# Row factors of a four-layer graph attention kernel: turned on TensorE ahead of DRAM, with a new set of due times

## The chip, the core and the metric

The kernel runs on one core of one Trainium2 chip. A core has five engines with a queue each: TensorE (PE in the profile, with its weight loads as PEld), VectorE (DVE), ScalarE (ACT), GpSimd (POOL) and SyncE (SP, which here only issues DMAs). The metric is the device time of one execution, in microseconds (us), as the median of the runs; lower is better. All data is float32.

## What is computed

Eight graphs (b = 0 to 7) of 2048 nodes with 128 channels share one symmetric 0/1 adjacency matrix. Four layers follow each other, and each is added to its input x:

```
h = relu(layernorm(x))
layer 0: Wh = h @ W.T;  s1 = Wh @ a1;  s2 = Wh @ a2
         e[i,j] = leaky_relu(s1[i] + s2[j], 0.2), only where adj[i,j] > 0
         x += elu(softmax(e) @ Wh)
layer 1: the same with Wh = h @ W and no elu
layer 2: 4 heads of 32 channels, scores = h_i . h_j, masked softmax, x += softmax @ h
layer 3: h scaled by node weights, Wh layer-normed, attention as in layer 0,
         x += elu(softmax(e) @ Wh + Wh)
```

In layers 0, 1 and 3 the score is a sum of one number of node i and one of node j, so exp(leaky_relu(s1 + s2)) is a maximum of two products. The kernel needs one factor per node as a column (a number for each partition) and another as a row that lies on all 128 partitions. This row is the "row factor" of the title.

## The kernel before

**Units and the two kinds of work.** There are 32 units, one per graph and layer. Layers 0, 1 and 3 are `Gat` units, layer 2 is a `Heads` unit. Both begin with a prelude: mean and variance of x (`moments`), normalised rows (`rows_made`, ACT), transposes on PE (`transposes`), and for a `Gat` unit the projections and `put` or `put3`, which leave the values `y` and the factors `cr` in SBUF.

The main work of a `Gat` unit is 32 *tokens* (two halves of the target nodes by 16 blocks of source nodes). One token is a DVE instruction `front` (line 718: maximum of the row factors `r` and a column of `cr`, times the edges) and a `back` on PE (line 727: 8 products of 128x128 by 128x129, which the profile counts as 16 matmul instructions). Three buffers `zg` lie between the two. In all there are 768 tokens.

The main work of a `Heads` unit is 64 *beats* (4 heads by 16 blocks): four score matmuls on PE (line 994), two exponentials on ACT (line 1001), a mask on DVE (line 1007) and a weighing on PE (line 1016), mostly for two beats at once. Five buffers `z` hold the beats, and two pairs of PSUM banks ("pair") are shared by the scores, all transposes and all projections. In all there are 512 beats.

**How the row factor gets to all partitions.** `spread` ends a `Gat` unit's prelude. `self.cr[:, 1, :]` holds 128 partitions by 16 numbers; node n*128+p lies on partition p, column n. For 21 of the 24 `Gat` units, `write` (line 667) sends it by DMA to a row of 2048 numbers in DRAM. `targets` (line 698) later reads each half of that row back onto all 128 partitions as `r`, by two DMAs for a unit; the first `front` of a half needs its `r`. The other three units, (0,0), (0,1) and (7,3), spread the row by PE transposes and ACT copies without DRAM (lines 650 and 659), and are not touched. A second way by DRAM stands in the code behind the flag `ROWS_TURNED` (lines 669 to 687).

**What sets the order.** The instruction order of each engine is written out ahead by a planner (`Plan`). Each `Op` has an engine, an estimated duration, needs, slots it takes and frees, a `lag` until others can use its result, and a `due` time. The planner goes through an estimated execution; among the operations of an engine that can start within `WINDOW_US` of the earliest one it takes the one with the lowest due. `HURRY_US` moves fronts ahead while more than one `zg` is free. Due times come from three tables: `TOKENS` (start and step for each unit and half; its order is also the order of all tokens, each bound to the one before it), `BEATS` (start and step for each graph and head; beats, too, are bound in one sequence), and `LEADS` (how long before its start a unit's prelude begins). `EARLY` shifts the kinds of operations against each other. `GATES` holds the tokens of unit (6,3) until named beats of graph 7. The tables give priorities, not times on the chip: waits on the chip come only from data, buffers and queue order.

SP issues in planned order as well: x loads, adjacency loads, the `halves` and `values` of a `Heads` unit to DRAM (lines 898 and 919) and back (933, 939, 944), row writes, row reads and the output. An SP instruction that waits holds up all behind it.

Of the kernel before, what the change touches and what calls it, by code (L numbers as in the profile page):

```python
# [20 lines left out]
P = 128  # L21
# [19 lines left out]
def adj_preln_d4(ctx: ExitStack, tc: tile.TileContext, x, adj, w0, a0, w1, a1, w3, a3,  # L41
# [114 lines left out]
            self.needs = [n for n in needs if n is not None]  # L156
            self.got, self.end, self.users, self.ready = {}, None, [], 0.0

    HURRY_US, WINDOW_US, BEAT_SUMS_US = 89.3, 0.131, 0.86

    EARLY = dict(front=-87.0, score=211.3, exp=171.0, mask=-122.3, sums=-168.7)

    SINGLY = (7,)
    FIRST_ALONE = 4
    DIRECT, ROWS_TURNED, L1_ACT, L3_DMA, L3_OUT = ((0, 0), (0, 1), (7, 1), (7, 2)), False, False, False, False
    PLUS_US, PLUS_LAG_US, GATHER_US, GATHER_LAG_US = 1.0, 5.5, 2.2, 6.5

    class Plan:
# [71 lines left out]
    def fast(ctx):  # L240
# [186 lines left out]
        class Unit:  # L427
# [15 lines left out]
            def moments(self, name, part, rows, needs):  # L443

                key = {}

                def stats(op, q):
                    if q == 0:
                        key["st"] = stat.tile([P, NB, 6], F32, tag="st", name="st")
                    for n in range(q * 4, q * 4 + 4):  # L450
                        nc.vector.bn_stats(out=key["st"][:, n, :], in_=rows()[:, n, :])  # L451

                def begin(op):
                    key["total"], key["v"] = moments_begin(stat, name, key["st"])

                def power(op):
                    key["rstd"] = moments_power(stat, name, key["v"])

                def end(op):
                    key["nmr"] = moments_end(stat, name, key["total"], key["rstd"])  # L460

                if (self.b, self.layer) == (0, 0):
                    return self.first_moments()
                last = []
                for q in range(4):
                    last = [add("DVE", 0.72, self.due(part + 0.03 * q), lambda op, q=q: stats(op, q),
                                last + list(needs[q]))]
                last = [add("DVE", 0.5, self.due(part + 0.11), begin, last)]
                last = [add("POOL", 3.4, self.due(part + 0.12), power, last)]
                return key, [add("DVE", 0.09, self.due(part + 0.14), end, last)] * 4  # L470

            def first_moments(self):

                key, ready = {}, []

                def stats(op, half):
                    if half == 0:
                        key["st"] = stat.tile([P, NB, 6], F32, tag="st", name="st")
                        key["rstd"] = stat.tile([P, NB], F32, tag="rstdx", name="rstdx")
                        key["nmr"] = stat.tile([P, NB], F32, tag="nmrx", name="nmrx")  # L480
                    for n in range(half * HB, (half + 1) * HB):
                        nc.vector.bn_stats(out=key["st"][:, n, :], in_=X[0][:, n, :])
                    sl = slice(half * HB, (half + 1) * HB)
                    key["total", half], key["v", half] = moments_begin(stat, "x", key["st"][:, sl, :])

                def power(op, half):
                    sl = slice(half * HB, (half + 1) * HB)
                    nc.gpsimd.tensor_tensor(out=key["rstd"][:, sl], in0=key["v", half], in1=neg_half[:, sl], op=OP.pow)

                def end(op, half):  # L490
                    sl = slice(half * HB, (half + 1) * HB)
                    nc.vector.scalar_tensor_tensor(key["nmr"][:, sl], key["total", half], -0.5, key["rstd"][:, sl],
                                                   op0=OP.mult, op1=OP.mult)

                for half in range(2):
                    last = add("DVE", 1.9, half, lambda op, half=half: stats(op, half), self.after)
                    last = add("POOL", 3.4, half, lambda op, half=half: power(op, half), [last])
                    last = add("DVE", 0.09, half, lambda op, half=half: end(op, half), [last])
                    ready += [last] * 2
                return key, ready  # L500
# [44 lines left out]
        class Gat(Unit):  # L545
# [92 lines left out]
            def spread(self):  # L638
# [30 lines left out]
                if ROWS_TURNED:  # L669
# [3 lines left out]
                        nc.tensor.transpose(ps[0:NB, op.got["pair"], :P], self.cr[:, 1, :], ident)  # L673

                    def copy_rows(op):
                        key["r"] = stat.tile([NB, P], F32, tag="rt", name="rt", bufs=2)
                        nc.scalar.copy(key["r"], ps[0:NB, turned.got["pair"], :P])

                    def write_rows(op):
# [206 lines left out]
        class Heads(Unit):  # L886
# [172 lines left out]

        GATES = {(6, 3, 0): (7, 10), (6, 3, 1): (7, 48)}  # L1060
        TOKENS = {
            (1, 0, 0): (97.6, 6.88), (0, 1, 0): (73.5, 14.16), (0, 1, 1): (550.6, 7.34),
            (1, 0, 1): (1660.4, 7.3), (2, 0, 0): (1689.5, 7.62), (2, 0, 1): (1764.4, 9.18),
            (1, 1, 0): (430.5, 13.69), (1, 1, 1): (1072.7, 7.7), (3, 0, 0): (1245.7, 8.98),
            (3, 0, 1): (1288.7, 8.31), (2, 1, 0): (1760.1, 7.68), (2, 1, 1): (872.6, 3.08),
            (0, 3, 0): (1689.1, 7.43), (0, 3, 1): (1912.1, 10.3), (3, 1, 0): (2530.9, 14.04),
            (4, 0, 0): (1726.7, 7.6), (3, 1, 1): (1682.5, 8.06), (4, 0, 1): (1756.3, 7.23),
            (1, 3, 0): (1633.1, 3.91), (1, 3, 1): (1288.3, 6.99), (4, 1, 0): (1701.6, 7.25),
            (4, 1, 1): (2745.4, 9.07), (5, 0, 0): (1716.2, 8.46), (5, 0, 1): (1683.8, 9.5),
            (2, 3, 0): (1952.7, 2.05), (2, 3, 1): (2876.6, 8.01), (5, 1, 0): (3026.3, 4.35),  # L1070
            (5, 1, 1): (3255.9, 7.54), (6, 0, 0): (3217.4, 3.78), (6, 0, 1): (3228.0, 6.29),
            (3, 3, 0): (3360.5, 9.13), (3, 3, 1): (3610.0, 7.36), (6, 1, 0): (3752.1, 13.03),
            (6, 1, 1): (4083.3, 4.99), (7, 0, 0): (4105.3, 7.44), (7, 0, 1): (4586.2, 9.82),
            (4, 3, 0): (4181.2, 4.29), (7, 1, 0): (4249.1, 11.6), (7, 1, 1): (4504.3, 7.29),
            (4, 3, 1): (4662.4, 11.71), (5, 3, 0): (4541.9, 11.87), (5, 3, 1): (4694.2, 12.84),
            (6, 3, 0): (4390.1, 14.25), (6, 3, 1): (5179.1, 7.43), (7, 3, 0): (5192.3, 8.4),
            (7, 3, 1): (6460.1, 7.89),
        }
        BEATS = {
            (0, 0): (-266.53, 15.11), (0, 1): (-315.14, 21.46), (0, 2): (-14.69, 14.66),  # L1080
            (0, 3): (593.67, 2.8), (1, 0): (-621.42, 13.74), (1, 1): (-215.39, 3.18),
            (1, 2): (-485.77, 7.14), (1, 3): (278.01, 8.1), (2, 0): (678.31, 14.14),
            (2, 1): (886.15, 2.23), (2, 2): (953.01, 2.45), (2, 3): (1726.79, 10.94),
            (3, 0): (-127.35, 10.64), (3, 1): (1129.71, 0.0), (3, 2): (1181.46, 7.17),
            (3, 3): (1316.42, 11.55), (4, 0): (1548.48, 23.99), (4, 1): (2361.91, 1.13),
            (4, 2): (2366.8, 7.55), (4, 3): (2544.1, 8.8), (5, 0): (2510.32, 10.6),
            (5, 1): (2257.53, 0.0), (5, 2): (2962.35, 15.09), (5, 3): (3457.98, 6.48),
            (6, 0): (2333.01, 6.11), (6, 1): (2924.65, 1.75), (6, 2): (3322.16, 3.55),
            (6, 3): (3721.7, 12.09), (7, 0): (2053.35, 4.55), (7, 1): (2736.5, 1.99),
            (7, 2): (3763.83, 3.23), (7, 3): (3926.73, 7.25),  # L1090
        }
        LEADS = {
            (0, 0): 691.08, (1, 0): 439.88, (0, 1): 835.27, (2, 0): 752.06, (1, 1): 991.07,
            (3, 0): 872.93, (2, 1): 1117.92, (0, 3): 876.91, (3, 1): 44.84, (4, 0): 102.77,
            (1, 3): 1841.07, (4, 1): 1823.39, (5, 0): 52.64, (2, 3): 756.18, (5, 1): 646.99,
            (6, 0): 832.07, (3, 3): 413.34, (6, 1): 340.77, (7, 0): 1416.38, (4, 3): 263.35,
            (7, 1): 510.12, (5, 3): 767.47, (6, 3): 756.1, (7, 3): 1090.32, (0, 2): 205.64,
            (1, 2): 1275.92, (2, 2): 878.78, (3, 2): -270.32, (4, 2): -845.43, (5, 2): 647.9,
            (6, 2): -738.75, (7, 2): -534.5,
        }  # L1100

        def planned():
# [18 lines left out]
            def there(b, layer):  # L1121
                if (b, layer) not in units:
                    if layer:
                        there(b, layer - 1)
                    if layer == 2:
                        start = BEATS[b, 0][0]
                        units[b, 2] = Heads(b, 2, start - LEADS[b, 2], start - 14.0)
                        units[b, 2].beats([BEATS[b, h] for h in range(HEADS)])
                    else:
                        start = next(TOKENS[name][0] for name in TOKENS if name[:2] == (b, layer))  # L1130
                        units[b, layer] = Gat(b, layer, start - LEADS[b, layer], start)
# [218 lines left out]
```

## Time and profile before

| | |
|---|---|
| median of 3 runs | 2776.76 us (2772.88 to 2777.48) |
| the profiled execution | 2775.01 us |
| its span, first to last instruction | 2773.2 us |
| granted PE clock over the span | 0.990 of full speed |
| DVE mask, line 1007, x512 | 1169.8 us, 2286 ns each |
| DVE front, line 718, x768 | 971.4 us, 1279 ns each |
| PE back, line 727, x12288 | 1499.0 us busy |
| PE scores, line 994, x2048 | 720.5 us busy |
| PE weighing, line 1016, x4096 | 502.6 us busy |
| ACT exponential, line 1001, x1024 | 1122.8 us, 1114 ns each |
| DMA packets, and those under 512 B | 255513, 185456 |
| DMA queue 1 (issued by SP) | 186784 packets, 156.46 MB, 23.4% of 16 engines |

Busy time of an engine is the time in which at least one of its instructions runs. Matmuls are pipelined, so that a duration of one is longer than the distance between two, and a PE that is busy all the time need not be at its fastest. The span is 1.8 us shorter than the execution's own time, for what lies before the first and behind the last instruction.

### The profile page before, as it was taken

The page shows a single profiled execution, that of the slowest core. Times are in us where ns is not written, and L with a number is a line of the kernel's source. Part 1 is how long each engine was busy: PE and PEld are TensorE (multiplying, and loading weights), DVE is VectorE, ACT ScalarE, POOL GpSimd, SP SyncE. Part 2 cuts the span into 40 slices and gives each one's busy share as a digit, 9 for nine tenths or more (in the row PEclk, how much of TensorE's full clock was granted, in tenths as well). Part 3 has the DMA queues.
Part 4 walks back from the last instruction along what each step waited for, and adds up shares of the span by engine and source line. Part 5 has one row for each costly group of instructions (what it writes and reads, how often), then busy time and mean ns, then how long its engine had stood idle before and what let it go on. Part 6 is the DMA issues. An engine that isn't in the chain of part 4 may idle for free. (4 is left out here: it accounts for less than half of the span.)

```text
span 2773.2 us, 48892 instructions
## 1 busy us (share of the span) xinstructions
PE 2632.3 (95%) x20083; PEld 2024.3 (73%) x20083; DVE 2515.8 (91%) x3323; ACT 1714.9 (62%) x2768; POOL 253.5 (9%) x114
## 2 busy tenths in 40 slices
PE   6999899999998999999999999999999899999987
PEld 6998778757775677877777678786777567665677
DVE  6867798989999899999999999999899899899987
ACT  4333566567666658656767567665676756787651
POOL 2100010011001001001100011010010100010010
PEclk9999999999999999999999999999999999999999
DMA  8005233432224424323333423423324221623000
GB/s 308 17 9 94 60 58 58 92 62 48 78 58 93 56 54 73 66 65 58 54 65 85 80 42 74 79 53 69 62 59 95 46 54 16 122 50 58 12 16 25
DMA packets 255513, 181.78 MB, mean 66 GB/s; under 512 B 185456, under 2 KB 220400, under 8 KB 249136
## 3 DMA queue, kind: packets, MB, share of 16 engines
q1 hardware_dynamic: 186784, 156.46, 23.4%
q0 software_dynamic: 68080, 22.04, 8.3%
q8 instruction: 159, 2.61, 0.4%
q14 instruction: 74, 0.61, 0.1%
q10 hardware_dynamic: 416, 0.07, 0.0%
HBM read 123.03 MB, written 33.73 MB: 57 GB/s over the span
## 5 line engine op out<-in xcount | busy, mean ns | idle before, releaser
L1001 ACT ACTIVATE z<-ps,shift 128x1024 f32<-128x1024 f32 x1024 | 1122.8, 1114 | 725.5 <-PE ps L994 719.5
L727 PEld LDWEIGHTS ps<-y,zg 128*128 128x128 f32 x12288 | 1466.7, 193 | 85.1 <-DVE zg L718 41.2
L727 PE MATMUL ps<-y,zg 128*128 128x129 f32 x12288 | 1499.0, 276 | 31.1 <-DVE zg L718 28.1
L1007 DVE SCALAR_TENSOR_TENSOR z<-z,edge 128x2048 f32<-128x2048 f32 x512 | 1169.8, 2286 | 70.0 <-ACT z L1001 68.6
L718 DVE SCALAR_TENSOR_TENSOR zg<-r,cr,edge 128x1024 f32<-128x1024 f32 x768 | 971.4, 1279 | 119.1 <-PE ps L727 98.3
L994 PE MATMUL ps<-m,s 128*128 128x512 f32 x2048 | 720.5, 438 | 66.2 <-ACT z L1001 55.1
L994 PEld LDWEIGHTS ps<-m,s 128*128 128x128 f32 x2048 | 314.9, 191 | 348.3 <-ACT z L1001 243.6
L1016 PE MATMUL ps<-z,v 128*32 128x512 f32 x4096 | 502.6, 602 | 2.2 <-DVE z L1007 1.8
L1016 PEld LDWEIGHTS ps<-z,v 128*32 128x32 f32 x4096 | 103.1, 109 | 238.6 <-issue 187.0
L511 ACT ACTIVATE h<-x,nmrx,rstdx 128x128 f32<-128x128 f32 x512 | 210.5, 491 | 47.9 <-DVE nmrx L116 31.9
L111 POOL TENSOR_TENSOR rstdx<-varx,neg_half 128x16 f32<-128x16 f32 x31 | 123.2, 3973 | 760.5 <-DVE varx L106 760.5
L1041 POOL DMA_DIRECT2D x<-o x31 | 65.8, 2123 | 838.8 <-DVE o L1036 748.8
L566 PEld LDWEIGHTS ps<-rhs,h_t 128*128 128x128 f32 x768 | 102.0, 199 | 9.2 <-ACT h_t L558 3.7
L566 PE MATMUL ps<-rhs,h_t 128*128 128x130 f32 x768 | 107.1, 285 | 0.3 <-ACT h_t L558 0.3
L451 DVE BATCH_NORM_STATS2 st<-x 128x6 f32<-128x128 f32 x496 | 106.7, 279 | 0.0
L540 PE MATMUL ps<-ident,h 128*128 128x128 f32 x512 | 81.2, 281 | 18.2 <-ACT h L511 11.1
L540 PEld LDWEIGHTS ps<-ident,h 128*128 128x128 f32 x512 | 63.0, 143 | 36.1 <-ACT h L511 13.2
L795 POOL DMA_DIRECT2D x<-oa x26 | 23.5, 903 | 665.4 <-DVE x L789 176.6
L766 ACT ACTIVATE oe<-oa 128x1024 f32<-128x1024 f32 x32 | 33.9, 1060 | 74.0 <-DVE oa L785 63.2
L760 DVE TENSOR_TENSOR oa<-ps,rs 128x384 f32<-128x384 f32 x144 | 73.9, 513 | 5.0
L558 ACT COPY h_t<-ps 128x512 f32<-128x512 f32 x96 | 55.9, 584 | 31.1 <-PE ps L540 31.1
L591 ACT ACTIVATE y<-ps,y 128x128 f32<-128x128 f32 x256 | 73.0, 369 | 0.0
(120 smaller groups left out, 818.9 us busy)
## 6 DMA issues: line engine op xcount, KB each, us to landing
s<-halves SPq DMA_DIRECT2D x256, 128.0 KB, 2.8
m<-halves SPq DMA_DIRECT2D x64, 512.0 KB, 6.9
r<-row SPq DMA_DIRECT2D x42, 512.0 KB, 4.1
raw<-in_adj_dram SPq DMA_DIRECT2D x16, 1024.0 KB, 16.7
x<-oa POOLq DMA_DIRECT2D x26, 512.0 KB, 5.2
values<-h SPq DMA_DIRECT2D x32, 256.0 KB, 2.5
halves<-hi SPq DMA_DIRECT2D x128, 64.0 KB, 1.7
halves<-lo SPq DMA_DIRECT2D x128, 64.0 KB, 1.7
```

The source lines that it names most:

```text
L111: nc.gpsimd.tensor_tensor(out=rstd, in0=v, in1=neg_half, op=OP.pow)
L451: nc.vector.bn_stats(out=key["st"][:, n, :], in_=rows()[:, n, :])
L511: nc.scalar.activation(self.h[q][:, k, :], X[self.b][:, n, :], AF.Relu, scale=key["rstd"][:, n:n + 1], bias=key["nmr"][:, n:n + 1])
L540: nc.tensor.transpose(pk[:, k, :], self.h[q][:, k, :], ident)
L566: nc.tensor.matmul(pv[:, k, :C + 2], lhsT=self.h_t[q][:, k * P:(k + 1) * P], rhs=rhs, start=True, stop=True)
L718: nc.vector.scalar_tensor_tensor(z, self.r[half], self.cr[:, 0, jb:jb + 1], edge[:, jb, half * HN:(half + 1) * HN], op0=OP.max, op1=OP.mult)
L727: nc.tensor.matmul(ps[:, self.banks(half, place)[i // 3], k * CE:(k + 1) * CE], lhsT=z[:, i * P:(i + 1) * P], rhs=self.y[:, jb, :], start= ...
L760: nc.vector.tensor_mul(key["a"][:, i0:i1, :], pv[:, :, :C], r[:, i0:i1, None].to_broadcast([P, i1 - i0, C]))
L994: nc.tensor.matmul(ps[:, lo + c, :], lhsT=self.S[h, jb // HB][:, at:at + P], rhs=self.M[h][:, (c2 * 2 + c) * 512:(c2 * 2 + c + 1) * 512], ...
L1001: nc.scalar.activation(self.z[s][:, c2 * HN:(c2 + 1) * HN], ps[:, lo:lo + 2, :].rearrange("p b t -> p (b t)"), AF.Exp, bias=shift)
L1007: nc.vector.scalar_tensor_tensor(self.z[s], self.z[s], 1.0, edge[:, jb, :], op0=OP.mult, op1=OP.mult, accum_out=self.den[:, h, jb:jb + 1])
L1016: nc.tensor.matmul(ps[c * HD:(c + 1) * HD, 0, :], lhsT=self.V[h][:, jb, :], rhs=z[:, c * 512:(c + 1) * 512], start=jb == 0, stop=jb == NB - 1,
```

## The change

`ROWS_TURNED` becomes True. The 21 units that sent the factors straight to DRAM now transpose them on PE into a PSUM bank (128 partitions by 16 columns become 16 partitions by 128), copy these by ACT into a tile `rt` of [16, 128] and write that. The row in DRAM has the same 2048 numbers in the same places, and the reading is the same. `rt` gets one buffer in place of two, and `st` (the statistics of a prelude) two in place of three. All numbers of `TOKENS`, `BEATS`, `LEADS`, `EARLY`, `HURRY_US` and `WINDOW_US` are new; in `TOKENS` the two halves of unit (2,1) now come ahead of those of unit (3,0), and the rest keeps its order. `there` makes the `Heads` unit of the graph before first, so that beats stay in the order of graphs. `GATES` stays.

```diff
-    HURRY_US, WINDOW_US, BEAT_SUMS_US = 89.3, 0.131, 0.86
-    EARLY = dict(front=-87.0, score=211.3, exp=171.0, mask=-122.3, sums=-168.7)
+    HURRY_US, WINDOW_US, BEAT_SUMS_US = 70.8, 0.139, 0.86
+    EARLY = dict(front=-107.6, score=111.1, exp=-8.6, mask=-164.7, sums=-334.5)
...
-    DIRECT, ROWS_TURNED, L1_ACT, L3_DMA, L3_OUT = ((0, 0), (0, 1), (7, 1), (7, 2)), False, False, False, False
+    DIRECT, ROWS_TURNED, L1_ACT, L3_DMA, L3_OUT = ((0, 0), (0, 1), (7, 1), (7, 2)), True, False, False, False
...
-                        key["st"] = stat.tile([P, NB, 6], F32, tag="st", name="st")
+                        key["st"] = stat.tile([P, NB, 6], F32, tag="st", name="st", bufs=2)
...
-                        key["r"] = stat.tile([NB, P], F32, tag="rt", name="rt", bufs=2)
+                        key["r"] = stat.tile([NB, P], F32, tag="rt", name="rt", bufs=1)
...
         TOKENS = {
-            (1, 0, 0): (97.6, 6.88), (0, 1, 0): (73.5, 14.16), (0, 1, 1): (550.6, 7.34),
-            (1, 0, 1): (1660.4, 7.3), (2, 0, 0): (1689.5, 7.62), (2, 0, 1): (1764.4, 9.18),
-            (1, 1, 0): (430.5, 13.69), (1, 1, 1): (1072.7, 7.7), (3, 0, 0): (1245.7, 8.98),
-            (3, 0, 1): (1288.7, 8.31), (2, 1, 0): (1760.1, 7.68), (2, 1, 1): (872.6, 3.08),
+            (1, 0, 0): (-22.6, 16.91), (0, 1, 0): (53.7, 14.45), (0, 1, 1): (278.3, 12.5),
+            (1, 0, 1): (1550.7, 12.7), (2, 0, 0): (1538.2, 13.82), (2, 0, 1): (1781.1, 13.31),
+            (1, 1, 0): (27.5, 13.73), (1, 1, 1): (467.0, 14.14), (2, 1, 0): (387.8, 14.31),
+            (2, 1, 1): (552.8, 14.26), (3, 0, 0): (1505.8, 15.6), (3, 0, 1): (544.1, 12.33),
...
         BEATS = {
-            (0, 0): (-266.53, 15.11), (0, 1): (-315.14, 21.46), (0, 2): (-14.69, 14.66),
+            (0, 0): (-186.75, 13.08), (0, 1): (-165.33, 21.31), (0, 2): (148.16, 8.98),
...
         LEADS = {
-            (0, 0): 691.08, (1, 0): 439.88, (0, 1): 835.27, (2, 0): 752.06, (1, 1): 991.07,
+            (0, 0): 491.95, (1, 0): 357.11, (0, 1): 1280.8, (2, 0): 1208.77, (1, 1): 234.77,
...
                     if layer == 2:
+                        if b:
+                            there(b - 1, 2)
                         start = BEATS[b, 0][0]
```

The branch that the flag turns on is already in the code before:

```
if ROWS_TURNED:
    key = {}
    def turn_rows(op):
        nc.tensor.transpose(ps[0:NB, op.got["pair"], :P], self.cr[:, 1, :], ident)
    def copy_rows(op):
        key["r"] = stat.tile([NB, P], F32, tag="rt", name="rt", bufs=2)
        nc.scalar.copy(key["r"], ps[0:NB, turned.got["pair"], :P])
    def write_rows(op):
        self.row = dram.tile([N], F32, name="row", bufs=4)
        nc.sync.dma_start(out=self.row.rearrange("(n p) -> n p", p=P), in_=key["r"])
    at = self.due(0.82 if self.layer == 3 else 0.9)
    turned = add("PE", 0.12, at, turn_rows, last, takes=["pair"])
    last = add("ACT", 0.25, at, copy_rows, [turned], frees=[("pair", turned)])
    self.written = add("SP", 0.5, at, write_rows, [last], lag=2.5)
    return
self.written = add("SP", 0.5, self.due(0.82 if self.layer == 3 else 0.9), write, last, lag=11.5)
```

The planner reckons the landing of a row write at 2.5 us in place of 11.5.

## The prediction

> **What bounds the kernel.** I read the busy times of the page first, then busy time in three stretches, then the waits of SP, and last the stretches in which no token runs.
>
> ```profile
> PE 2632.3 (95%) x20083; PEld 2024.3 (73%) x20083; DVE 2515.8 (91%) x3323; ACT 1714.9 (62%) x2768; POOL 253.5 (9%) x114
> ...
> 0.00:290.00 290.00, 251.41 (x2147) 240.14 (x2147) 211.02 (x379) 103.39 (x314) 35.87 (x26) 0.98 0.40 111
> 290.00:2637.00 2347.00, 2271.34 (x17020) 1678.50 (x17021) 2197.11 (x2788) 1566.38 (x2347) 209.95 (x86) 0.99 0.33 63
> 2637.00:2773.00 136.00, 109.52 (x918) 105.62 (x916) 107.72 (x157) 45.10 (x107) 7.64 (x2) 0.92 0.07 21
> ```
>
> A window row gives start:end, length, then busy us of PE, PEld, DVE, ACT and POOL, the clock, the DMA share and GB/s. The first line is the whole span: PE is idle for 141 us, DVE for 257. The first beat starts at 290.5 us, the last score at 2637. Ahead of that only tokens run and PE sets the pace (idle 38.6 us, most of it in the first 60 us and around 250 to 290). In the middle PE is idle for 75.7 us and DVE for 149.9: two engines close to full, so an order that mixes tokens (PE 16 instructions, about 1.8 us, one front of 1.28 us) and beats (mask 2.29 us) evenly is worth something, and nothing that loads PE is free. At the end PE is idle for 26.5 us.
>
> **What the row write does now.** In the DMA issues a row write of 8 KB takes 11.4 us to land, and a store of 64 KB takes 1.7; SP's waits say who stands behind it.
>
> ```profile
> row<-cr SPq DMA_DIRECT2D x21, 8.0 KB, 11.4
> halves<-hi SPq DMA_DIRECT2D x128, 64.0 KB, 1.7
> ...
> SPq L698 <- DMA row<-cr: 130.3, 14, 11.9
> ```
>
> The reader is to see that bytes are not the cost: the write is 2048 pieces of 4 bytes, and SP stood for 130.3 us in 14 reads until a row had landed. The timeline of SP shows two ways in which this hurts (start, duration, what):
>
> ```profile
> 234.09 0.46 SPq L667 DMA_DIRECT2D row<-cr  x1
> 235.32 2.03 SPq L919 DMA_DIRECT2D halves<-hi  x4
> 237.45 10.28 SPq L919 DMA_DIRECT2D halves<-lo  x4
> ...
> 577.27 0.38 SPq L667 DMA_DIRECT2D row<-cr  x1
> 588.00 1.07 SPq L698 DMA_DIRECT2D r<-row  x2
> ```
>
> First, the issue of four stores behind a row write takes 10.28 us where four such stores take 1.7 to 2.0: the prelude of the first `Heads` unit is held by 8.4 us. Second, the read of the row follows its write 10.7 us later, and the unit's tokens wait for it. Counting 16 matmuls of line 727 per token, no token runs in four stretches that contain a row write for the next unit, or follow it at once:
>
> ```profile
> 566.00:601.00 35.00, 29.06 (x151) 13.35 (x151) 29.99 (x51) 25.69 (x31) 5.81 (x2) 0.90 0.30 76
> 820.00:856.00 36.00, 27.76 (x157) 12.50 (x155) 31.50 (x35) 29.37 (x41) 2.10 (x1) 1.00 0.60 117
> 918.00:944.00 26.00, 21.69 (x127) 10.31 (x125) 21.54 (x24) 19.85 (x26) 0.93 (x1) 1.00 0.56 61
> 2384.00:2411.00 27.00, 21.70 (x116) 9.33 (x115) 20.49 (x23) 25.77 (x42) 0.00 (x0) 0.94 0.82 161
> ...
> 1311.00:1387.00 76.00, 76.00 (x593) 58.75 (x592) 74.92 (x122) 57.10 (x95) 10.73 (x5) 1.00 0.28 51
> ```
>
> PE is idle there for 124 - 100.2 = 23.8 us. The last row is the contrast: tokens and beats flow, and PE is full.
>
> **The change, part by part.**
>
> *1. The write.* It becomes 16 pieces of 512 bytes from 16 partitions. Nearest row: the 64 KB stores of `halves`, 1.7 us. The Trainium skill speaks against the new shape (SBUF — State Buffer, "Door 1: The DMA port swizzle" and "The DMA setup-cost knee"): transfers should span 128 partitions, since partitions 0 to 15 reach 4 of 16 ports, some 109 GB/s; and each DMA has about 2 us that bytes don't change. By that rule 8 KB take 2 + 8192 B / 109 GB/s = 2.1 us (an estimate), by the row 1.7. Both are far below 11.4, and no transfer here is wide enough for the ports to matter; I take 2.0. The chain from factors to `r` gains 9.4 us, less the transpose and the copy with their handovers, 0.8 us: 8.6 us per unit. In the four stretches that is 34 of 124 us, and with the idle time in proportion 0.28 x 23.8 = **6.6 us**. Bounds: 0, if the read is then late for another cause (at 846.3 the read itself took until 856 beside an x load); 23.8, if the stretches close. In the other 17 units tokens of earlier units cover the latency; nothing is gained, and what is late next is the prelude's own ACT work.
>
> *2. The queue.* The stores at 237.45 go through in about 2 us. DVE waited 5.28 us for them and PE 2.74 right after; later PE waits 9.43 us for the first m load. The first beat can come 8 us earlier. I take **4 us**: the 2.74 and a little of the 9.43, which is also the queue of s and m loads itself. Bounds 0 and 12.2. Packets fall by 21 x 2048 = 43,008.
>
> *3. The added work.* Per unit one transpose with 16 stationary columns on PE, one ACT copy of 16x128, and a PSUM pair held in between. PE: four transposes of line 540 take 0.60 us and one 0.28, so 0.11 us each; 21 x 0.11 = 2.3 us, at full price, as PE has no cover. ACT: a copy of 512 columns out of PSUM is 0.59 us and an activation of 4 columns is 0.18; 128 columns lie at 0.285 us, 6.0 us for 21. ACT is 62% busy, so most of it is hidden behind exps that wait for PE; but the copy stands in line ahead of exps, and the pair is one of two that the scores need (about 0.9 us each time). I take 4 us for both; bounds 0, and 6 + 19 = 25 if every hold delays a score in full. Sum: **6.3 us** lost.
>
> *4. Buffers.* One `rt`: a copy waits only if the last write has not been read out; the closest two row writes are 61.9 us apart (1083.7 and 1145.6), so nothing. Two `st`: DVE writes and reads it in its own order, so nothing; if preludes are drawn together, a few tenths. The new line in `there` moves no beat, since the graphs come in order already.
>
> *5. The due times.* The trace cannot show the new order. Gain is bounded by PE's idle time in the middle and around the first beat: 75.7 + 14.8 (gaps of 2.74, 2.64 and 9.4 us) - 10.6 already counted = 80 us. Here a rule decides how far one may go: the Trainium skill (Perfetto Trace Analysis, "Identifying the Most-Contended Engine") says that matmul busy time is no measure of headroom and LDWEIGHTS busy time is. By it PE has 27% left, 749 us. But in the full stretch 1311 to 1387 PEld is at 58.75/76 = 77% with PE never idle: that is this mix at its pace. From 73.0 to 77.3% is 5.6% of the span, 155 us, close to the 141 of idle time. So I keep the row's ceiling. Loss is bounded by the two emptiest middle slices: PE has 61 of 69 or 70 us at 832 to 901 and at 2149 to 2219, 8 to 9 idle where an average slice has 2; four more like them cost 28 us. The start (load of x and adjacency) and the end (same `GATES`, and nothing but graph 7's last unit) stay. Both ends are far apart; nearest is the better half of the middle itself: slices like 1317 to 1387 show that the order can be tight, and a search that plans with 2.5 us instead of 11.5 may put a unit's tokens where droughts were. I take a quarter of the ceiling, **20 us**.
>
> Sum against the profiled execution: 2775.0 - 6.6 - 4 + 6.3 - 20 = 2750.7. The median stands 1.75 above that execution: 2752.
>
> **Rivals.**
>
> *B, the new order closes most gaps.* Droughts vanish and two thirds of the ceiling go: 23.8 + 4 - 6.3 + 38 = 60 us, 2717. For it: two engines have their work in 2516 and 2632 us and still need 2773. Against it: the old order was planned with the same lists, and the sequence of units hardly changes. Chance 0.22 (2700 to 2735).
>
> *C, slower: exps come late on ACT.* `EARLY` puts exps 180 us later against the preludes (171.0 to -8.6), so where both are ready ACT takes rows first: 256 groups of four activations at 1.1 to 1.7 us a group (lines 511, 518, 591, 631). Each can hold a PSUM pair and with it the next score. For it: weight loads of scores already wait 243.6 us for exps, PE itself 55.1. If a group costs PE 0.25 us, that is 64 us, and 2752 + 64 = 2816; with the direct losses it decides from 0.09 us a group, where 24 us are gone. Against it: ACT is idle for 38% and its exps wait 719.5 us for scores. Chance 0.18 (2782 to 2816).
>
> *D, nothing much:* the row latency is already covered and the new order is as good as the old, 2770 to 2782. Chance 0.12, of which 0.07 within 0.2% (5.6 us, about what these measurements can tell from no change).
>
> **How the numbers follow.** Likeliest, 0.48: 2752, own range 2735 to 2770. The 8-in-10 range takes in most of B and half of C: 2710 to 2790. Faster by over 0.2%: 0.48 + 0.22 + 0.05 = 0.75; within: 0.07; slower: 0.18.
>
> **What would show it.** Right: row writes land in about 2 us; packets near 212,800, under 512 B near 142,450; the wait of reads for rows from 130 to below 40 us; 21 new transposes and copies near 0.3 us; stretches without tokens shorter or gone; first score before 285 us; PE idle near 118 us. Wrong: droughts of the same length with another cause; PE waits for exps well over 55 us (C); DVE idle under 200 us (B); row writes that land above 5 us, which would take parts 1 and 2 away.

## The result, and the profile after

The changed kernel takes 2751.72 us in the median of 6 runs (2748.61 to 2757.35), the kernel before 2773.99 us in 6 runs beside it (2772.0 to 2777.48). The ratio is 0.992 with a 95% interval of 0.9907 to 0.9933: about 22 us less. Forecast was 2752, or 24 us less than the profiled execution of the kernel before. The sum came out, but not as closely as the two times look: the kernel before was 2.8 us faster in these six runs than in the three that the forecast was worked out from, and two terms of the sum were off in opposite directions, as the experiments show.

Page, DMA issues and SP's waits of the kernel after:

```profile
PE 2626.4 (96%) x20104; PEld 2020.1 (74%) x20104; DVE 2515.0 (92%) x3323; ACT 1720.2 (63%) x2789; POOL 261.7 (10%) x114
...
DMA packets 212842, 181.80 MB, mean 66 GB/s; under 512 B 142448, under 2 KB 177728, under 8 KB 206464
```

```profile
row<-rt SPq DMA_DIRECT2D x21, 8.0 KB, 1.5
```

```profile
SPq L698 <- DMA row<-rt: 32.6, 20, 3.3
```

The span is 2746.8 us. PE is idle for 120.4 us of it (140.9 before) and busy for 5.9 us less. A row write lands in 1.5 us in place of 11.4, 43,008 packets of 4 bytes are gone, and SP's reads wait 32.6 us for rows in place of 130.3.

The same span in stretches, cut where the first score starts and the last ends:

```profile
0.00:230.00 230.00, 207.10 (x1775) 196.73 (x1776) 172.12 (x320) 88.63 (x278) 30.56 (x24) 0.99 0.28 101
230.00:274.00 44.00, 40.07 (x347) 38.82 (x346) 36.59 (x56) 11.76 (x30) 3.63 (x3) 1.00 0.60 150
274.00:2615.00 2341.00, 2274.55 (x17121) 1683.66 (x17120) 2204.20 (x2797) 1574.62 (x2374) 220.82 (x87) 1.00 0.30 64
2615.00:2746.80 131.80, 104.69 (x868) 100.85 (x867) 102.07 (x152) 45.16 (x107) 6.73 (x2) 0.91 0.06 18
```

The first score comes 17 us earlier (273.5 in place of 290.5), with 105 tokens done in place of 107. Up to there PE's idle time falls from 38.6 to 26.8 us; in the middle it goes from 75.7 to 66.4, at the end from 26.5 to 27.1. So half of the idle time that went lay ahead of the first score.

The stretches without tokens did not close:

```profile
563.00:602.00 39.00, 31.04 (x172) 14.69 (x171) 31.78 (x53) 29.84 (x48) 7.94 (x3) 0.96 0.55 109
817.00:858.00 41.00, 33.44 (x195) 15.78 (x194) 34.86 (x37) 34.43 (x59) 0.35 (x1) 1.00 0.36 84
...
2353.00:2384.00 31.00, 24.96 (x135) 9.98 (x134) 24.90 (x32) 29.35 (x46) 0.00 (x0) 0.94 0.70 177
```

Three of the four are there still, at 39, 41 and 31 us where they were 35, 36 and 27. Only the one before 944 shrank (926 to 934), and one of 24 us, from 1220 to 1244, is new.

At the first beat the timeline of PE shows it best. Before, and after:

```profile
290.49 1.19 PE L994 MATMUL ps<-m,s 128*128 128x512 f32 x2 [9.43 <-DMA m<-halves]
```

```profile
273.50 0.73 PE L994 MATMUL ps<-m,s 128*128 128x512 f32 x2 [1.77 <-DMA m<-halves]
```

PE stood for 9.43 us until an m had landed; now it stands for 1.77. Which m that was, the line does not say. The instruction's semaphores do: before, they were those of the *second* set of s and m loads, issued at 279.0 to 281.4, and not of the first, issued at 266 to 271. The program's SP sequence gives the reason. By the old due times head 1 of graph 0 starts at -315 and head 0 at -267, so SP loaded head 1 first, while the beats run head 0 first. By the new ones (-187 and -165) head 0 comes first.

### The profile page after: what moved, and what is told of

It reads as the page before. It is cut to its first block, busy times and chain, and to the rows that moved or that the text cites. A ratio compares the mean times of both kernels' runs of the same rounds, so it can differ in the third digit from the quotient of the medians.

```text
span 2746.8 us, 48941 instructions
## 1 busy us (share of the span) xinstructions
PE 2626.4 (96%) x20104; PEld 2020.1 (74%) x20104; DVE 2515.0 (92%) x3323; ACT 1720.2 (63%) x2789; POOL 261.7 (10%) x114
## 5 line engine op out<-in xcount | busy, mean ns | idle before, releaser
L994 PE MATMUL ps<-m,s 128*128 128x512 f32 x2048 | 721.1, 438 | 63.6 <-ACT z L1001 59.1
L111 POOL TENSOR_TENSOR rstdx<-varx,neg_half 128x16 f32<-128x16 f32 x31 | 130.3, 4204 | 643.9 <-DVE varx L106 643.9
```

Of the source, the lines that this page charges most:

```text
L111: nc.gpsimd.tensor_tensor(out=rstd, in0=v, in1=neg_half, op=OP.pow)
L994: nc.tensor.matmul(ps[:, lo + c, :], lhsT=self.S[h, jb // HB][:, at:at + P], rhs=self.M[h][:, (c2 * 2 + c) * 512:(c2 * 2 + c + 1) * 512], ...
```

## The experiments

Theory: the short row write gives some 10 us, the new due times the rest. Rivals: the write is hidden and the due times give everything; or a few single places give all. Times in us below are the distance of the ratios times 2774. In e1, e2, e5, e6 and e8 the order on every engine stays exactly as it was, so that nothing but the named part differs; in e9, e10 and e11 SP alone exchanges three pairs of loads.

### Row write alone, in either order

```diff
 # e1: the kernel after, its order, transposes and copies kept
-nc.sync.dma_start(out=self.row.rearrange("(n p) -> n p", p=P), in_=key["r"])
+nc.sync.dma_start(out=self.row.rearrange("(n p) -> p n", p=P), in_=self.cr[:, 1, :])
 # e2: the kernel before, its order kept; e8 the same, for unit (2,0) alone
-nc.sync.dma_start(out=self.row.rearrange("(n p) -> p n", p=P), in_=self.cr[:, 1, :])
+nc.sync.dma_start(out=self.row.rearrange("(p n) -> p n", n=NB), in_=self.cr[:, 1, :])
```

> The changed kernel with its order, transposes and ACT copies kept, but the row is written from cr in 2048 pieces of 4 bytes, as before. If the short write carries the gain under the new order (W): rows land in about 11 us again where 2.5 were planned, stores behind them take 10 us to issue, the first score comes 8 us later, and 10 us or more come back: 2762 us or above. If the new order alone carries it and the write is hidden (O): within 3 us of the changed kernel, 2749 to 2755.

> The kernel before with its order kept on every engine, and only the row write changed: 128 pieces of 64 bytes, without transposes or copies; the row then has its nodes in another order, so row factors go to other targets. W as the prediction put it (parts 1 and 2): 10 us less, 2764. Rival P: with the order of DVE and PE fixed no stretch without tokens can close, so only part 2 shows, around the first beat: 3 to 6 us less, 2768 to 2771, and the four stretches stay at 35, 36, 26 and 27 us. O: no change, 2774.

> The kernel before with its order kept, and only the row write of unit (2,0), the one at 234 us ahead of the first Heads unit's stores, in 128 pieces of 64 bytes (its row factors go to other targets). If the gain of the short write under the old order lies around the first beat (P): the same time as with all 21 writes short, 3 to 6 us less than before. If it lies elsewhere: no change from before.

Measured: e1 0.9992 of before (0.9985 to 0.9998), e2 0.9961 (0.9948 to 0.9974), e8 0.9983 (0.9976 to 0.9991). In the old order the short writes give 10.8 us (7 to 14), which is W and more than P's 3 to 6; the single one ahead of the first `Heads` unit's stores gives 4.7 of these. In the new order the write is worth 20 us: without it nearly nothing is left of the change. The write is not hidden, and the new order needs it. But the first score of e1 starts at 276.4, only 2.9 us later and not 8: SP stands in the read of the row first, and the stores behind that read issue in 1.8 to 2.2 us.

Where it acts is seen when the start of each token and score is compared with its like in the kernel of the same order. In e2 6.4 us are won from the tokens at 251 to the first score at 290, 5.0 at the tokens from 856 on, and elsewhere single steps of 1 to 2.5 us up and down. In e1 5.0 us are lost at 255, 4.9 at 602, 3.5 at 1090. Timeline of SP in e8, of the stores that took 10.28 us before, and SP's wait in the kernel before:

```profile
232.06 0.46 SPq L668 DMA_DIRECT2D row<-cr  x1
233.30 1.74 SPq L922 DMA_DIRECT2D halves<-hi  x4
235.14 1.79 SPq L922 DMA_DIRECT2D halves<-lo  x4
```

```profile
SPq L919 <- DMA row<-cr: 11.8, 2, 8.7
```

The four stores issue in 1.79 us once the row write ahead of them has 128 pieces and not 2048. In the kernel before, three of them went out in 1.3 us and the fourth stood for 8.7 us (the longest of the two waits) until the row had landed. It does not read the row. The trace shows why it waits: SP's DMAs count on eight semaphores in turn, and this store is the eighth DMA behind the row write, so it takes the semaphore that the row write still holds. The two longest stretches without tokens, in e2:

```profile
814.00:846.00 32.00, 26.83 (x154) 12.07 (x153) 30.78 (x34) 27.25 (x40) 2.10 (x1) 1.00 0.72 160
560.00:594.00 34.00, 28.08 (x152) 12.60 (x150) 29.37 (x51) 25.93 (x32) 5.81 (x2) 0.95 0.31 85
```

One gave 4 us, the other 1; the remaining two stayed within 2 us. With DVE's order written out, a row that lands earlier starts a front earlier only where that front was waiting. The waits of e1 show the reverse, on SP and on DVE:

```profile
SPq L698 <- DMA row<-cr: 206.1, 21, 12.7
```

```profile
DVE zg L718 <- DMA r<-row: 14.7, 6, 5.2
```

All 21 reads now stand behind a row, and fronts wait 14.7 us for `r`, where they waited 9.1 us in the kernel before and no front waits for it in the kernel after.

### Which head is loaded first

```diff
 # e9: the kernel before; e10: e9 with the short write of e2; e11: the kernel after
 plan.run()
+for k in (0, 2, 3):      # s, m and v of heads 0 and 1 of graph 0
+    i, j = (plan.order.index(ops[k]) for ops in first_loads)
+    plan.order[i], plan.order[j] = plan.order[j], plan.order[i]
```

> The kernel before, order kept, but SP loads s, m and v of graph 0's head 0 ahead of those of head 1 (the old due times had head 1 at -315 and head 0 at -267, so head 1 was loaded first, while the beats run head 0 first). If this is what PE waited 9.43 us for (L): the first score comes at 281 in place of 290, when its tokens are done, and 6 to 9 us go: 0.997 of before. If SP's queue and the busy DMA engines are it: no change.

> The kernel before, order kept, with head 0 loaded first and the row writes in 128 pieces of 64 bytes (row factors go to other targets). L: what head order brings adds to what the short write brings, less where both act on the same first beat: first score at 274 to 276, 0.993 to 0.995 of before, so that the old order with these two comes within 6 us of the changed kernel. If both remove the same wait: no better than the short write alone, 0.996.

> The changed kernel, order kept, with graph 0's head 1 loaded ahead of head 0, as it was before the change. L: the first score waits for the second m load, about 8 to 10 us later than 273.5, and 5 to 9 us come back: 2757 to 2761. If the load order is not it: no change.

Measured: e9 0.9969 (0.9957 to 0.9981), e10 0.9929 (0.9915 to 0.9942), e11 0.999 (0.9983 to 0.9997). PE at the first score in e9 and in e11:

```profile
282.29 0.71 PE L996 MATMUL ps<-m,s 128*128 128x512 f32 x2
```

```profile
284.94 1.19 PE L996 MATMUL ps<-m,s 128*128 128x512 f32 x2 [13.97 <-DMA m<-halves]
```

In e9 PE goes from tokens to the score without a stop, 8.2 us earlier than before. In e11 it stands for 13.97 us, 11.4 later than in the kernel after; the rest of e11's 19 us, which is over twice what was expected, comes in steps of 1 to 3 us later on; why the loss grows there is open. Swapping three load operations, with no change to what is computed, is worth 8.6 us in the old order.

e10 is the experiment that decides: head order and short write add (0.31% + 0.39%, measured 0.71%), its first score starts at 274.5, and the *old* order with these two lies within 3 us of the changed kernel, 0.9929 against 0.992. Its row factors stand at other targets, and it has no transposes and copies, which cost the changed kernel some 2.5 us (next section).

### The added work

```diff
 # e5: the kernel after, its order kept; the row written as in e2
-nc.tensor.transpose(ps[0:NB, op.got["pair"], :P], self.cr[:, 1, :], ident)
-nc.scalar.copy(key["r"], ps[0:NB, turned.got["pair"], :P])
+pass
 # e6: each of the two five times
+for _ in range(5):
```

> The changed kernel with its order kept on every engine but without the 21 transposes and 21 ACT copies; the row is written from cr in 128 pieces of 64 bytes, so its nodes lie in another order and row factors go to other targets. The prediction's part 3: the added work costs 6.3 us, so 2745. Rival: ACT's gaps and PE's waits hide nearly all of it, at most the 2.3 us on PE are won: 2749 to 2752.

> The changed kernel with each of the 21 transposes and copies made five times in place of once. Part 3 at 6.3 us a set: 4 x 6.3 = 25 us more, 2777. Rival, hidden work: PE 4 x 2.3 = 9 us more at the most and ACT nothing, 2752 to 2761.

Measured: e5 0.9903 (0.9885 to 0.9921), e6 0.9956 (0.994 to 0.9973). Four more sets cost 10 us, 2.5 each (0.5 to 4.6 from the ends of the intervals). The 25 us of part 3 are excluded. Taking the one set out wins 4.7, which these intervals can't tell from 0 or from 6.3. The tile `rt` in the kernel after:

```profile
L677 ACT COPY rt<-ps x21: 237/238/257, 53.5 to 2502.3; 16x128 f32<-16x128 f32 x21
```

A copy is 238 ns; the 21 waited for their transposes 2.7 us in all, and the one wait that the trace puts down to a copy is a weight load's of 0.8 us. So the hold of the pair delays little.

### Flag and due times apart, and a nudge to the plan

```diff
 # e3: before, ROWS_TURNED True, st and rt as in the change   # e4: after, ROWS_TURNED False
 # e12: the kernel after
-self.written = add("SP", 0.5, at, write_rows, [last], lag=2.5)
+self.written = add("SP", 0.5, at, write_rows, [last], lag=3.5)
```

> Old due times with ROWS_TURNED on (rt one buffer, st two), planned anew with the lag of 2.5 us. W: direct parts of the prediction, 10.6 less and 6.3 more, 2770. O: no gain or a loss, since the due times were found for the other lag: 2774 to 2795.

> New due times with ROWS_TURNED off, planned anew with the lag of 11.5 us and the row written as before. O: most of the gain stays, 2750 to 2760. W: about 4 us above the changed kernel by the direct parts, 2756; if the due times hold only together with the short lag (T): 2770 or above.

> The changed kernel planned anew with 3.5 us in place of 2.5 for the landing of a row write, nothing else. If the new due times suit short writes in general (T): within 6 us of the changed kernel. If they suit only the one estimated execution that they were searched with (F): 10 to 60 us more, as when flag and due times were mixed.

Measured: e3 1.0182 (1.0169 to 1.0195), e4 1.0217 (1.0204 to 1.023), e12 1.0099 (1.0084 to 1.0114). Each *loses* 27 to 60 us against before, e3 more than either side expected, and e12 is 50 us slower than the kernel after though 1 us of one estimated latency is its only edit (F). Two stretches without tokens, and what follows the last score, in e12:

```profile
564.00:610.00 46.00, 36.94 (x199) 17.10 (x198) 36.98 (x61) 35.38 (x56) 7.97 (x3) 0.93 0.51 103
840.00:912.00 72.00, 59.45 (x321) 25.13 (x320) 64.53 (x102) 57.35 (x81) 10.55 (x3) 0.98 0.37 82
2663.00:2799.40 136.40, 98.23 (x782) 91.46 (x780) 90.89 (x137) 40.29 (x97) 5.82 (x2) 0.86 0.04 13
```

Stretches of 46 and 72 us stand where the kernel after has 39 and 41, and the first token behind the second one starts 54 us later (912 in place of 858). The end is not to blame: it takes 136 us in place of 132. So the comparison of a flag with fixed due times measures the plan's fragility and not the flag: e3 and e4 say nothing of what the short write is worth, while e1 and e2 do.

### Without transposes, by a strided read

```diff
 # e7: the row written by half, partition and column; new due times, flag off, lag 2.5
+for half in range(2):
+    nc.sync.dma_start(out=self.row[half * HN:(half + 1) * HN].rearrange("(p n) -> p n", n=HB),
+                      in_=self.cr[:, 1, half * HB:(half + 1) * HB])
...
+z.rearrange("p (n t) -> p n t", t=P), r.rearrange("p (t n) -> p n t", n=HB),
```

> New due times, planned with the lag of 2.5 us, without transposes and copies: each half of the row is written in 128 pieces of 32 bytes, so that it lies in DRAM by partition and then column, and DVE's front reads r with a stride of 32 bytes. If a strided fp32 operand costs DVE nothing, fronts stay at 1.28 us and the time is that of the changed kernel less up to 6 us, give or take a new order: 2740 to 2765. If DVE pays for the stride, fronts get longer, and 672 of them carry it: at 0.1 us each 67 us more.

Measured: 1.1498 (1.1479 to 1.1518), 3195 us. The fronts, strided (line 727 there) and plain (line 723):

```profile
L727 DVE SCALAR_TENSOR_TENSOR zg<-r,cr,edge x672: 2004/2111/2207, 109.6 to 3073.0; 128x1024 f32<-128x1024 f32 x168
L723 DVE SCALAR_TENSOR_TENSOR zg<-r,cr,edge x96: 1266/1283/1289, 37.7 to 3174.1; 128x1024 f32<-128x1024 f32 x96
```

A strided front takes 2.11 us and not 1.28; 672 of them load DVE by some 556 us more. The order is new too, and a new order alone moved the time by up to 60 us above, so the 0.83 us of a front is the firm figure here, and the time of the run is not. The transposes at 2.5 us for all are the cheap way.

## Why the prediction came out, step by step

**1, the write: right in size, wrong in place.** It lands in 1.5 us (forecast 2.0, from estimates of 1.7 and 2.1), near the row of 1.7 that it was priced by. The 6.6 us came from shortening all four stretches in proportion, by 34 us. e2 shortens them by some 5 us, nearly all in one: their length is set by the order that DVE was given. In the kernel after three of the four are longer, so the sign "droughts of the same length with another cause" came true. The agreement of 10.8 us (e2) with 6.6 + 4 is partly luck of the places.

**2, the queue: right in size.** 4 us were forecast for the write ahead of the first stores; e8 has 4.7 (2.5 to 6.7). The line of 10.28 us was read as slow issue of four stores; it was one store's wait of 8.7 us for the row's semaphore.

**3, the added work: too dear.** 6.3 us forecast, 2.5 (0.5 to 4.6) by e6, about what part 3 put on PE alone. Most of the 4 us for ACT's line and the pair was not there, and the rival's bound was the better price.

**5, the due times: the step that was read wrong.** 20 us were forecast as a general tightening, a quarter of the 80 us of PE's idle time. From the runs it is 22.2 - 10.8 + 2.5 = 14 us, and 8.6 of these are one thing, the order in which two heads are loaded. The step failed at the 9.43 us of PE: part 2 put them down to "the queue of s and m loads itself" and took only a little of them, and part 5 left the rest in the ceiling as idle time like any other, though the due times of head 1 (-315) ahead of head 0 (-267) stood in the diff. That 20 was too much by 6 and the added work too dear by 4 nearly cancelled in the sum. The rest of the new tables, among them unit (2,1) ahead of (3,0), is 5 us by this sum. By e5, the new order without the added work (0.9903), against e10, the old order with both repairs (0.9929), it is 7; the intervals of these two meet, so that its size is not known well. That the two repairs also lose 20 us each when undone in the new order shows that its gain is not a sum of theirs: the new order leaves no room where the old one had some. What in it does so is open.

**Rivals.** B, stretches closing: did not happen. C, late exps: PE's wait for them is 59.1 us after and 55.1 before, no change of note. D: no.

## What to carry to other kernels

When a list scheduler's inputs change, every order changes, so an A/B of one feature through the planner can be off by more than the feature is worth; freeze the order and swap the one operation to price it. When an engine waits for a DMA, look up which transfer its semaphores count before blaming the queue: here the right data was loaded second, and swapping three issues gave 8.6 us. And a transfer of few bytes in thousands of pieces is paid by what stands behind it: the read of what it wrote, the stores queued after it, and the DMA that takes its semaphore next.

## What the runs showed of the hardware

A write of 8 KB lands in 11.4 us as 2048 pieces of 4 bytes, in 1.5 us as 128 pieces of 64 bytes, without any transpose, and in 1.5 us as 16 pieces of 512 bytes. In the trace of before a packet of 4 bytes on SP's queue takes 7 ns in the median, and the 54,944 of them 34 us of each of the 16 engines, so the packets' own time is far from 11 us a write. Stretches of the kernel before, behind the row write at 577.27, where SP issued nothing until the row had landed at 588, and behind the one at 234.09, with seven stores after it:

```profile
580.00:587.00 7.00, 5.44 (x28) 1.90 (x27) 7.00 (x13) 6.14 (x6) 0.00 (x0) 1.00 0.02 1
240.00:245.00 5.00, 5.00 (x48) 5.00 (x47) 3.23 (x3) 0.00 (x0) 0.00 (x0) 1.00 0.95 18
```

When the write is alone, its last packet starts 2.7 us after the issue, and the DMA engines are idle (share 0.02) for most of the time until it lands. With stores behind it, the engines count as 0.95 busy while only 18 GB/s move, and the seven stores land late too; these lines give the time from their issue to landing before, and of all eight in e8:

```profile
DMA to landing us min/median/max: 10.8/11.3/11.9
```

```profile
DMA to landing us min/median/max: 1.6/1.6/1.6
```

So this write in 2048 pieces held up the stores behind it for about as long as itself. What the delay consists of is open.

DVE's three-operand instruction on float32 was slower when one operand was read with a stride of 32 bytes: 2.11 us for 1024 columns in place of 1.28. In e7 all three operands were addressed as 8 runs of 128, two of them without gaps; what that does alone was not run.

A wait of 9.4 us also costs after it. Windows of the kernel before, around the first score:

```profile
285.00:290.00 5.00, 0.00 (x0) 0.00 (x0) 0.00 (x0) 0.00 (x0) 0.00 (x0) 0.50 1.03 155
290.00:295.00 5.00, 4.51 (x23) 4.24 (x24) 0.00 (x0) 3.13 (x6) 0.00 (x0) 0.60 0.02 4
```

The granted clock (third number from the end) falls to 0.50 and 0.60, and the 16 matmuls of a token at 292.33 take 2.76 us, where at full clock they take 1.95. In e9, where PE does not wait there, the clock reads 1.00 in both windows and the token behind the first score takes 1.95 us; in the kernel after, with a wait of 1.77 us, it is 1.00 as well.
